# Splitting one long score product in the pair phases and adding met waits on TensorE: a causal attention layer on one core

## Chip, cores and metric

The kernel runs on one core of a Trainium2 chip. The metric is the device time of one execution in microseconds; lower is better. The engines are named as the profile names them: PE (TensorE matmuls), PEld (its weight loads), ACT, DVE, POOL and SP (which issues transfers).

## The reference

The input is x of 32 x 256 x 32 x 32 in float32, that is 32 batches of 256 channels and 1024 positions. It is normalised in 32 groups of 8 channels, then goes through a causal attention of 8 heads of 32 channels without the diagonal, and the result is added to x.

```python
q = jnp.einsum('oc,bcs->bos', q_w, xf) + q_b[None, :, None]
kv = jnp.einsum('oc,bcs->bos', kv_w, xf) + kv_b[None, :, None]
...
mask = jnp.tril(jnp.ones((S, S), dtype=x.dtype), -int(MASK_CENTER))
scores = jnp.einsum('bhqd,bhkd->bhqk', q, k) / jnp.sqrt(jnp.asarray(dk, x.dtype))
scores = jnp.where(mask == 0, jnp.asarray(-10000.0, x.dtype), scores)
attn = jax.nn.softmax(scores, axis=-1)
attn = jnp.where(mask == 0, jnp.asarray(0.0, x.dtype), attn)
out = jnp.einsum('bhqk,bhkd->bhqd', attn, v)
...
x = x + _L0_conv_ref(_gn(x), L0_conv_q_w, L0_conv_q_b, L0_conv_kv_w, L0_conv_kv_b)
```

## The kernel before

A batch is worked through in 12 visits: two groups `g` of four heads, six visits each (the table `VISITS`). Everything is unrolled, and the order of instructions on each engine is that of the program, written out by hand in the loop over `i` at the end: visit `i` of batch `b` issues the scores of this visit, then what stands in the list `at` for it (one projection unit of this or the next batch), then the products with the values of the visit before (`values`), then sums of exponentials on DVE and other small work.

Scores. Keys stand on the partitions of the result, queries in its columns. Each product (`score`, L311) has 32 rows (one head's channels) and 64 keys, so that four heads (row groups) and two halves of a key block (column groups) make eight parts of the array. A visit has "longs", made by `full`, of up to 512 query columns, and "shorts". In six visits (numbers 1, 3, 4, 7, 9, 10) there is one long of 512 columns, and the shorts are a `pair`: two key blocks on the diagonal, each half in two products, of 128 and of 64 columns. Visits 0 and 6 are pairs as well, with two longs, of 384 and 128 columns. Three PSUM tiles take a visit's scores: `pairs[0]` (longs of heads 0, 1), `pairs[1]` (longs of heads 2, 3) and `pairs[2]` (all shorts).

Order within the scores (`scores`, from L348). First the shorts of heads 2, 3 (`first`); where the visit is in `PAIRS` and has two longs, one long of heads 0, 1 is put between its two parts and the parts are turned round (L364, L365). Then what remains of the longs of heads 0, 1 (`begin`), then a long of heads 2, 3. Then PE waits for the semaphore `bank_free`, which the last products of `first` raise, because the shorts of heads 0, 1 write the same banks; then these shorts. ACT takes the exponentials of the three tiles into SBUF (L397, L393), and POOL masks the diagonal ones (L339).

Projections. A unit is `project_qk` (a half of q or k for a group: two times four matmuls of 512 columns, `product`, L169, tile pp) or `project_v` (four times four matmuls of 256 columns, tile ppv). A batch has twelve units, one a visit, dealt by `PROJECT`; by the visit's number they are q or k in visits 7, 8, 10, 0, 1, 2, 5, 6 and v in 9, 11, 3, 4. `product` makes four matmuls of 32 result rows each, one for each column group of the array.

Values. `values` (L422) makes three or four times four matmuls of 128 to 512 columns into the tile acc.

Small work that PE has besides: `norm_mean` (tile pm, behind the values of visit 3) and `norm_variance` (pv, visit 4) for a later batch. SP waits for `bank_free` in `with_scores` to time some of its transfers. `ALIGN` places drains on DVE and 64 met waits on POOL (L669) at the start of the program. The semaphore `arrived` is at 1 or above from the load of the weights on.

## Time and profile before

| | |
|---|---|
| time, median of 3 runs | 1793.67 us (1793.61 to 1793.85) |
| the profiled execution's own time | 1793.44 us |
| its span, first to last instruction | 1791.7 us |
| granted TensorE clock, mean | 0.999 |
| PE busy | 1784.4 us, 37,036 matmuls |
| PEld busy | 948.2 us, 37,036 loads |
| DVE busy | 1673.4 us |
| ACT busy | 1456.4 us |
| POOL busy | 881.3 us |

A float32 matmul of the program stands in the trace as two, each with a weight load of its own, so counts of matmuls are twice those of the code. In the groups of instructions, `L311 PE MATMUL sT<-q,k 32*64 32x128` is a matmul from line 311 into tile sT, with 32 rows and 64 columns of weights and 128 moving columns. "x" gives the count, then follow busy time and mean length. A matmul's start is measured, its end is modelled. "Idle before" is time in which the engine did nothing ahead of the instruction, with what ended it; for PEld this is no loss, since loads run beside matmuls. In a table of stretches, each row is a stretch from A to B, its length, and for an engine the busy time and in brackets the number of instructions under way in it, then the granted clock, the share of the DMA engines and their rate. Sequencer instructions such as waits (EVENT_SEMAPHORE) have records but count as neither busy nor idle.

### The profile page before, as it was taken

What the parts mean: (1) busy time and instruction counts of PE and PEld (TensorE: products, weight loads), DVE (VectorE), ACT (ScalarE), POOL (GpSimd) and SP (SyncE); (2) the same over time, 40 slices, a digit from 0 to 9 for tenths busy, and PEclk for the clock granted to TensorE, in tenths of its full rate; (3) what the DMA queues carried; (4) which work ended last, traced back from release to release, by engine and by line L of the source; (5) the groups of instructions that cost most, each with busy time, mean ns of one, the idle gap of its engine ahead of it and who ended that gap; (6) DMA issues with size and microseconds to landing.
All of it is one profiled execution on the core that took longest, in us unless ns stands there. A gap on an engine that the chain in (4) does not pass through costs nothing.

```text
span 1791.7 us, 81825 instructions
## 1 busy us (share of the span) xinstructions
PE 1784.4 (100%) x37036; PEld 948.2 (53%) x37036; DVE 1673.4 (93%) x1826; ACT 1456.4 (81%) x1990; POOL 881.3 (49%) x903
## 2 busy tenths in 40 slices
PE   9999999999999999999999999999999999999998
PEld 5555555555555555555555555555555555555554
DVE  4689999999999999999999999999999999999998
ACT  6888878888788888788887888878888878888785
POOL 2345544554545555445554455454555544555452
PEclk9999999999999999999999999999999999999999
DMA  2566766767667766766676676767776667666664
GB/s 70 105 115 137 134 134 129 147 135 143 127 126 149 140 138 134 135 139 138 139 135 131 129 150 132 145 125 128 149 141 135 136 134 138 139 139 137 132 107 106
DMA packets 86818, 236.77 MB, mean 132 GB/s; under 512 B 21312, under 2 KB 22336, under 8 KB 70592
## 3 DMA queue, kind: packets, MB, share of 16 engines
q0 software_dynamic: 15872, 97.53, 40.1%
q1 hardware_dynamic: 70448, 133.89, 25.5%
q8 instruction: 290, 4.75, 1.1%
q14 instruction: 64, 0.52, 0.1%
q10 hardware_dynamic: 144, 0.07, 0.0%
HBM read 66.85 MB, written 34.57 MB: 57 GB/s over the span
## 4 chain that ended last, share of the span: by engine, by line
PE 99%; ACT 0%; DVE 0%; issue 0%; POOL 0%; POOLq 0%
PE sT L311 31%; PE acc L422 28%; PE pp L169 26%; PE ppv L169 13%; PE pd L474 1%; PE busy L155 0%; ACT e L397 0%; PE pv L169 0%; PE pm L169 0%; PE wt L148 0%; DVE rb_last L547 0%; ACT eh L393 0%; DVE rb_last L534 0%; DVE turned L531 0%; DVE acc L544 0%
## 5 line engine op out<-in xcount | busy, mean ns | idle before, releaser
L339 POOL TENSOR_SCALAR_AFFINE_SELECT diagonal<-eh 128x512 f32<-128x512 f32 x512 | 632.5, 1256 | 841.5 <-ACT eh L393 840.9
L397 ACT ACTIVATE e<-sT 128x1024 f32<-128x1024 f32 x768 | 744.4, 1022 | 250.3 <-PE sT L311 225.9
L440 DVE TENSOR_TENSOR e<-e,e 128x1024 f32<-128x1024 f32 x314 | 574.2, 1829 | 24.5 <-ACT v L275 3.2
L311 PE MATMUL sT<-q,k 32*64 32x128 f32 (+2 forms) x18432 | 578.4, 372 | 0.1
L311 PEld LDWEIGHTS sT<-q,k 32*64 32x64 f32 x18432 | 394.8, 131 | 188.4 <-PE sT L311 69.6
L169 PE MATMUL pp<-xn,wT 128*32 128x512 f32 x4096 | 492.2, 598 | 0.0
L422 PE MATMUL acc<-e,v 128*32 128x512 f32 (+3 forms) x4608 | 401.0, 450 | 0.0
L393 ACT ACTIVATE eh<-sT 128x768 f32<-128x768 f32 (+1 forms) x384 | 341.7, 890 | 0.0
L422 PEld LDWEIGHTS acc<-e,v 128*32 128x32 f32 x4608 | 149.2, 110 | 261.5 <-issue 238.9
L169 PE MATMUL ppv<-wT,xn 128*32 128x256 f32 x4096 | 247.5, 382 | 0.0
L440 DVE TENSOR_TENSOR diagonal<-diagonal,e 128x1536 f32<-128x1536 f32 x126 | 195.0, 1548 | 16.8 <-PE acc L422 9.2
L169 PEld LDWEIGHTS pp<-xn,wT 128*32 128x32 f32 x4096 | 107.0, 109 | 195.7 <-issue 163.7
L440 DVE TENSOR_TENSOR e<-e,eh 128x1024 f32<-128x1024 f32 x126 | 164.2, 1303 | 6.5
L422 PEld LDWEIGHTS acc<-diagonal,v 128*32 128x32 f32 x4096 | 121.1, 110 | 87.6 <-issue 76.0
L440 DVE TENSOR_TENSOR e<-e,diagonal 128x2048 f32<-128x2048 f32 x63 | 144.2, 2289 | 19.8 <-POOL diagonal L339 19.8
L169 PEld LDWEIGHTS ppv<-wT,xn 128*32 128x32 f32 x4096 | 120.1, 109 | 79.7 <-issue 7.0
L422 PE MATMUL acc<-diagonal,v 128*32 128x128 f32 x4096 | 158.7, 273 | 0.0
L244 ACT ACTIVATE xn<-x,shift,rstd 128x256 f32<-128x256 f32 x248 | 136.8, 608 | 0.6 <-POOL shift L229 0.6
L544 DVE TENSOR_TENSOR num<-num,rb 128x512 f32<-128x512 f32 x124 | 123.3, 994 | 0.2 <-DMA rb<-inverses 0.2
L453 POOL DMA_DIRECT2D e<-e x124 | 103.3, 833 | 38.2 <-issue 38.2
L547 DVE SCALAR_TENSOR_TENSOR rb<-num,v_bias_col,x 128x256 f32<-128x256 f32 x248 | 117.5, 515 | 4.4
L453 POOL DMA_DIRECT2D diagonal<-diagonal x124 | 104.1, 839 | 4.8 <-issue 4.8
(84 smaller groups left out, 984.4 us busy)
## 6 DMA issues: line engine op xcount, KB each, us to landing
x<-in_x_dram SPq DMA_DIRECT2D x124, 256.0 KB, 3.7
diagonal<-diagonal POOLq DMA_DIRECT2D x62, 512.0 KB, 5.4
e<-e POOLq DMA_DIRECT2D x62, 512.0 KB, 5.9
rb<-inverses SPq DMA_DIRECT2D x124, 256.0 KB, 3.9
out_dram<-rb SPq DMA_DIRECT2D x124, 256.0 KB, 4.9
diagonal<-diagonal POOLq DMA_DIRECT2D x62, 256.0 KB, 4.6
folded<-diagonal SPq DMA_DIRECT2D x62, 256.0 KB, 5.1
e<-e POOLq DMA_DIRECT2D x62, 256.0 KB, 5.0
```

The costliest lines, as they stand in the source:

```text
L169: nc.tensor.matmul(out[part], lhsT=lhsT[:, part], rhs=rhs, start=start, stop=stop, skip_group_check=True)
L244: nc.scalar.activation(to, of, AF.Identity, bias=live["shift", b][:, g : g + 1], scale=rstd)
L311: return nc.tensor.matmul(bank[c : c + KEYS, cols], lhsT=live["k", b, g][rows, kb * P + c : kb * P + c + KEYS], rhs=live["q", b, g][rows, ...
L339: nc.gpsimd.affine_select(out=square[:, :, place + s * P : place + (s + 1) * P], in_=raw[:, :, (1 - s) * KEYS : (3 - s) * KEYS], pattern=[ ...
L393: exp = nc.scalar.activation(eh.rearrange("p (n bank) q -> p bank n q", n=2)[:, :, :, :narrow], short[:, :, :, :narrow], AF.Exp)
L397: nc.scalar.activation(e[:, 2 * a : 2 * a + 2, :wide], pairs[a][:, :, :wide], AF.Exp)
L422: nc.tensor.matmul(acc[HD * j : HD * (j + 1), of], lhsT=live["v", b][:, kb, h * HD : (h + 1) * HD], rhs=e[:, j, :], start=first, stop=last ...
L440: nc.vector.tensor_add(to, to, tile_of(b, g, at))
L453: nc.gpsimd.dma_start(out=total[:rows], in_=total[rows : 2 * rows], accum_op=ALU.add)
L474: nc.tensor.matmul(pd[HD * j : HD * (j + 1), of], lhsT=pick, rhs=e[:, j, :], start=start, stop=stop, skip_group_check=True,)
L544: nc.vector.tensor_mul(num, num, rb)
L547: nc.vector.scalar_tensor_tensor(blocks(rb, s), blocks(num, s, (start + s) % 2 == 1), v_bias_col[:, g : g + 1], blocks(xt[:, g, cols], s), ...
```

## The change

Two things are changed. In the visits of `SPLIT` (1, 3, 4, 7, 9, 10, the six pairs with one long), the long of heads 0, 1 is issued in two pieces by `part_of`: columns 0 to 128 and columns 128 to 512. `begin` then has two entries, so that the branch of L364 is taken: the shorts of heads 2, 3 come with their second part first, the piece of 128 columns stands between their parts, and the piece of 384 columns follows them. The long of heads 2, 3 and the shorts of heads 0, 1 are as they were.

And `fill(k)` puts waits on PE for the semaphore `arrived`, which has long been reached, behind each group of four matmuls of a projection: twice the number that `FILL` has for this visit's place in the batch and the group's place `k` in the unit. It does so from visit 6 of the program on, there with `EXTRA` = 7 more. The numbers of `FILL` add up to 158, so that a batch has 316 wait statements.

```diff
+        def fill(k):
+            i = live.get("visit", -1)
+            if i >= SKIP:
+                for _ in range(2 * (sum(FILL[i % N][k : k + 1]) + EXTRA * ((i, k) == (SKIP, 0)))):
+                    nc.tensor.wait_ge(live["arrived"], 1)
...
@@ project_qk, behind each of the two products
+                fill(cc)
...
@@ project_v, behind each of the four products
+                    fill(NG * s + cc)
...
+        def part_of(b, g, bank, entry, of):
+            at, _, halves = entry
+            for j in (0, 1):
+                for ((c, kb, first, _, cols),) in halves:
+                    score(b, g, bank[:, j, :], j, (
+                        c, kb, first + of.start, of.stop - of.start, slice(cols.start + of.start, cols.start + of.stop)
+                    ))
...
-            if i in PAIRS and len(longs) > 1:
+            if v in SPLIT:
+                begin = [lambda n=n: part_of(b, g, pairs[0], longs[0], n) for n in (slice(0, P), slice(P, HALF))]
+            if i in PAIRS and len(begin) > 1:
                 first = short_of((2, 3), begin.pop(0), slice(None, None, -1))
             else:
                 first = short_of((2, 3))
...
+        SPLIT = 1, 3, 4, 7, 9, 10
...
+        FILL = ((8, 8), (8, 8), (8, 8), (4, 4, 4, 4), (3, 4, 4, 2), (1, 8), (8, 8), (8, 8), (8, 8), (0, 0, 0, 0), (0, 8), (4, 4, 4, 4))
+        SKIP, EXTRA = 6, 7
...
             for i in range(B * N + 1):
+                live["visit"] = i
                 if i < B * N:
                     scores(*divmod(i, N))
```

## The prediction

> **What bounds the kernel.** I read the page first: busy time and the chain that ended last.

> ```profile
> PE 1784.4 (100%) x37036; PEld 948.2 (53%) x37036; DVE 1673.4 (93%) x1826; ACT 1456.4 (81%) x1990; POOL 881.3 (49%) x903
> ...
> PE 99%; ACT 0%; DVE 0%; issue 0%; POOL 0%; POOLq 0%
> PE sT L311 31%; PE acc L422 28%; PE pp L169 26%; PE ppv L169 13%; PE pd L474 1%; PE busy L155 0%; ACT e L397 0%; PE pv L169 0%; PE pm L169 0%; PE wt L148 0%; DVE rb_last L547 0%; ACT eh L393 0%; DVE rb_last L534 0%; DVE turned L531 0%; DVE acc L544 0%
> ```

> TensorE is the chain, in three phases a visit: scores (sT), a projection (pp or ppv), products with the values (acc). The view of PE's waits holds 3.0 us in all, at the two ends of the run, so no engine is waited for in between. ACT ends the three exponentials of a visit at least 160 ns before the next visit overwrites their banks (visits 2 and 8; elsewhere 0.3 us or more). A saving on PE is therefore a saving in the end, and so is a loss.

> Next, the timeline of the weight loads over two visits of batch 12, columns start, length, what. The first visit is number 0, which already has its phases interleaved; the second is number 1, a pair without.

> ```profile
> 679.84 0.58 PEld L311 LDWEIGHTS sT<-q,k 32*64 32x64 f32 x40 [0.20 <-ACT v L275]
> 681.26 0.16 PEld L169 LDWEIGHTS pp<-xn,wT 128*32 128x32 f32 x8
> 684.41 0.54 PEld L311 LDWEIGHTS sT<-q,k 32*64 32x64 f32 x32 [0.41 <-ACT k L258]
> 685.81 0.16 PEld L169 LDWEIGHTS pp<-xn,wT 128*32 128x32 f32 x8
> ```

> The score phase takes 1.42 us in visit 0 and 1.40 in visit 1 (1419 and 1403 ns to the nanosecond). Over batches 2 to 29 every visit repeats within 2 ns; a batch is 55.09 us. Visits 1, 3, 7, 9, 10 have 1403 ns of scores, visit 4 has 1411. Third, matmuls of L311 under way in small windows from the start of each phase:

> ```profile
> 679.84:679.87 0.03, 0.02 (x4) 1.00 0.00 0
> 679.84:679.90 0.06, 0.05 (x8) 1.00 0.00 0
> 684.41:684.43 0.03, 0.02 (x4) 1.00 1.31 328
> 684.41:684.46 0.05, 0.05 (x4) 1.00 1.04 287
> 684.41:684.49 0.09, 0.08 (x8) 1.00 0.96 265
> ```

> Heads 2, 3 begin at 1 ns in both. Heads 0, 1, on other rows of the array, have begun within 55 ns in visit 0 (single starts: 28 to 48 ns), but in visit 1 not by 50 ns (55 to 75). That lag is what the first part of the change can take.

> [...] in visit 1 heads 0, 1 are 32 instructions behind the first of heads 2, 3 in the program, yet start before heads 2, 3 make their second pass at 162 ns. [...] from the end of the last score stream to the next phase's first load are 88 ns, in visits 0, 1 and 2 alike. [...]

> ```profile
> q8 instruction: 290, 4.75, 1.1%
> ```

> That is 16.4 KB a packet, and 290 times 256 is 74,240, near PE's 74,072 loads and matmuls. [...]

> **Part 1, the split, 192 times (6 visits, 32 batches).** Four products of 512 columns become four of 128 and four of 384: 48 more matmuls and 48 more loads a batch as the trace counts them (two passes for each). Columns stay the same. The order becomes that of visit 0: 64 columns of heads 2, 3; 128 of heads 0, 1; 128 of heads 2, 3; 384 of heads 0, 1; the long one of heads 2, 3; then the short ones of heads 0, 1 behind the bank_free wait. Two row streams run side by side, and I follow both with visit 0's starts.

> Heads 0, 1. In visit 1 their short products start at 964 ns and the last stream ends at 1258 + 57 = 1315, then 88 of drain: 1403. In visit 0 they start at 942: 27 ns less lag, about 5 lost on the extra passes. With the same 294 + 57 + 88 that makes 1381, a gain of 22.

> Heads 2, 3. In visit 0 the weight loads of their long product stand at places 64 to 79 of the phase, and come at 280, 356, 373, 390 ns for the four tiles, where visit 1, with places 48 to 63, had all four at 329 to 349. So the tiles start at 387, 409, 426, 443 (load to stream 53). At 512 columns the second pass follows 430 later, at 873 for the last, ends at 1303, plus 88 is 1391. This stream now ends last: **the phase is 1391, a gain of 12 ns**. Visit 4, which follows the small product pm, has 8 more of lag in heads 0, 1; I take half of it back. 5 x 12 + 16 = 76 ns a batch, x 32 = 2.43 us. Bounds: 0 (if the later loads slip by another 12) and 28 a visit with visit 4 at 36 (all of the lag, 5.6 us). No gain below nothing is likely: it would need the loads of heads 2, 3 later than in visit 0, whose first 64 instructions are the same.

> Nothing else moves by more: the exponential of heads 0, 1 comes some 20 ns sooner (visit 0: 1188, visit 1: 1210); bank_free rises at 566 instead of 564 ns, so SP's queued loads and stores stay where they were. DVE's and POOL's work hangs on ACT.

> **Part 2, the met waits.** By the diff there are 2 x 158 = 316 wait statements a batch from visit 6 on. On POOL the 64 statements of L669 left 32 records, two waits in each, and PE has single waits at L169:

> ```profile
> L669 POOLq EVENT_SEMAPHORE  x32: 42/43/43, 4.3 to 7.0; - x32
> L169 PEldq EVENT_SEMAPHORE  x67: 51/51/51, 7.2 to 1693.0; - x67
> ```

> So 158 instructions a batch, 31 x 158 + 16 + 7 = 4921 in all. Their spacing on PE is not in the trace. Bounds: 87 ns as on POOL (2.7 us over 31 steps), and 121, adding the 34 by which PE's single record (51) exceeds POOL's (17). I take 87 to 110. What they cost depends on the sequencer's lead. The waits of L169 before pm run 1.70 us ahead of their own matmuls, those before pv 1.27: 36 instructions ahead in both. By that rule the first wait behind a projection's first 16 instructions runs at some 965 ns of the visit, while the array is busy with scores until 1391.

> Visits with q or k: 8 waits, 16 instructions, 8 waits, then the loads of acc, due at about 3024 (110 before acc at 3134, as acc stands 1.74 us behind pp now). Instructions come at 17 ns for four (the steps 356, 373, 390). 965 + 70 + 16 E is below 3024 for E up to 124 ns: **hidden under the projection's 1.74 us**. Visits with v and 16 waits (3, 11): 965 + 270 + 16 E against 3034 (acc 1.75 us behind ppv): hidden up to E = 112. Visit 4 has 13, visit 9 none, 10 has 8: more room. Queued behind the waits are only PE's own loads and matmuls, and ACT, which waits for these; both are late only if the array is. I take nought. If the cover is gone the cost is 16 ns a visit for each ns of E above 112. A gain I exclude: no step of the array waits for a slower sequencer.

> **Fetch.** A batch now has 2306 PE instructions (2304 loads and matmuls, 2 waits), nine blocks and two. With 96 and 158 more it has 2560, ten blocks, so the crossings stay in place from batch to batch. Before they drifted by 2 a batch, and only once did a crossing show: in batch 25, visit 0, five weight loads come 64 ns late, hidden in 84 ns of slack ahead of their matmuls. I book nothing; bound, one exposed crossing a batch, 64 x 31 = 2.0 us. Thirty more fetches of 16 KB on a DMA share of 0.6 to 0.7 are nothing.

> **Sum.** 1793.44 is the profiled execution (span 1791.7, 1.7 around it), 0.23 under the median. 1793.44 - 2.43 = 1791.0; on the median, **1791.2 us**, -0.14%. About 0.2% (3.6 us) is what a measurement of this kernel can tell from no change.

> **Rivals.**
> A, chance 0.48: as above, 1790.0 to 1792.5.
> B, 0.28: the loads of heads 2, 3 don't slip, the whole 22 to 28 ns come: 192 x 22 = 4.2 us, to 5.6: 1788.0 to 1789.5. For it: the slip is seen in visit 0 alone. Against: the same 64 instructions stand before it.
> C, 0.15, slower: waits take over 112 ns each and the queue runs dry in visits 3 and 11. At 121 acc is late by 9 x 16 = 144 ns in each: 2 x 144 x 31 = 8.9 us, less 2.4: 1800. It decides from E = 118 (0.2% slower). Against: POOL's 87. For: PE's longer record.
> D, 0.09: the change doesn't do what it says in time, the lag only moves to the tail of heads 2, 3, or a crossing a batch eats it: 1792.5 to 1795.

> Faster by over 0.2% (under 1790.1) takes B and 0.05 of A: 0.33. Slower (over 1797.3) is C: 0.15. The rest 0.52. The range 1788.0 to 1795.0 leaves out C and the edge of B.

> **What would show it.** Right: score phases of visits 1, 3, 7, 9, 10 at about 1391 ns, heads 0, 1 starting at 28, heads 2, 3 ending last; visits 0, 2, 5, 6, 8, 11 unchanged; batch 55.02 us; some 4921 wait records on PE under 112 ns apart, the lead kept; 38,572 matmuls and about 321 fetches. B: phases near 1381. Wrong: acc starting later after ppv in visits 3 and 11 than the 1.75 us of before (C), or any visit's time varying from batch to batch.

## The result and the profile after

The changed kernel takes 1816.68 us (median of 4, 1813.36 to 1819.98) against 1793.76 us of the kernel before beside it: a ratio of 1.0127, 95% interval 1.0106 to 1.0148. It is 1.3% slower; forecast were 1791.2 us and a range up to 1795.0. The profiled execution took 1818.47 us.

The page of the changed kernel, beside the lines of the same rows in the prediction:

```profile
PE 1799.1 (99%) x38572; PEld 964.2 (53%) x38572; DVE 1669.3 (92%) x1826; ACT 1457.9 (80%) x1990; POOL 869.7 (48%) x903
...
q8 instruction: 322, 5.28, 1.2%
...
PE 99%; issue 1%; ACT 0%; DVE 0%; POOL 0%; POOLq 0%
...
L169 PE MATMUL pp<-xn,wT 128*32 128x512 f32 x4096 | 503.4, 598 | 7.8 <-issue 7.8
```

The last of these groups in the kernel before:

```profile
L169 PE MATMUL pp<-xn,wT 128*32 128x512 f32 x4096 | 492.2, 598 | 0.0
```

PE is still the chain, the counts (38,572 matmuls; 322 packets of instructions for about 321) are as forecast, and yet 1% of the chain is now "issue": PE stood still for nothing that the profile shows. The group of pp has 7.8 us of it where the kernel before had none; its busy time rose too, from 492.2 to 503.4 us, because a matmul's end is modelled and some ends reach into the gap (by 0.59 us from the last start in batch 5 below). So busy and idle together give the loss (19.0 us there), not the idle alone. The waits of PE say where:

```profile
PE pp L169 <- issue: 7.8, 10, 1.1
PE acc L442 <- issue: 2.0, 4, 0.8
```

**The split did what it should.** Timeline of the weight loads in visits 0 and 1 of batch 12, undisturbed here (start, length, what):

```profile
686.06 0.57 PEld L320 LDWEIGHTS sT<-q,k 32*64 32x64 f32 x40 [0.20 <-ACT v L284]
...
687.47 0.16 PEld L169 LDWEIGHTS pp<-xn,wT 128*32 128x32 f32 x8
...
690.62 0.57 PEld L320 LDWEIGHTS sT<-q,k 32*64 32x64 f32 x40 [0.41 <-ACT k L266]
...
692.01 0.16 PEld L169 LDWEIGHTS pp<-xn,wT 128*32 128x32 f32 x8
```

Visit 1 now looks like visit 0: 40 loads at once, and the projection 1.39 us behind the start of the scores. Scores take 1387 ns in the median in all six split visits; before they took 1403, in visit 4 1411. Small windows from the start of the phase, matmuls of L320:

```profile
690.62:690.65 0.03, 0.03 (x4) 0.03 (x4) 1.00 0.44 137
690.62:690.67 0.05, 0.04 (x7) 0.05 (x7) 1.00 0.58 164
```

By 50 ns seven are under way, where the kernel before had four: heads 0, 1 begin at 28 ns instead of 55.

**The waits did what they should.** The instructions of line 251:

```profile
L251 PEldq EVENT_SEMAPHORE  x4921: 51/51/51, 47.8 to 1785.9; - x197
```

4921 records of two waits each, as counted; within a group most of them (3506 of 4273 steps) follow each other by 105 or 106 ns, inside the 87 to 110 taken; the others by up to 146. In an undisturbed visit they cost nothing that shows: a batch without a disturbance takes 54.98 us, against 55.09 before, and 54.98 too when the waits are left out (split_only below).

**But not every batch is undisturbed.** Before, each batch took 55.09 us. Now they take 54.98 to 57.7 us, and the surplus has two places. I take the shortest time of each of the twelve visits as undisturbed, and add up over batches 1 to 30 what the visits have above it ("surplus" from here on): 18.7 us in visit 5, 8.3 in visit 0, 0.7 in all others; 27.7 in all. An undisturbed run would be 1793.44 - 32 x 0.11 = 1789.9 us; with the 27.7 it is 1817.6, of 1818.47 measured.

Here is one disturbed visit 5, that of batch 5: weight loads of PE in the timeline.

```profile
320.47 0.16 PEld L169 LDWEIGHTS pp<-xn,wT 128*32 128x32 f32 x8 [0.20 <-issue]
320.93 0.12 PEld L169 LDWEIGHTS pp<-xn,wT 128*32 128x32 f32 x3 [0.30 <-issue]
321.36 0.12 PEld L169 LDWEIGHTS pp<-xn,wT 128*32 128x32 f32 x3 [0.31 <-issue]
323.17 0.14 PEld L169 LDWEIGHTS pp<-xn,wT 128*32 128x32 f32 x2 [1.69 <-issue]
324.01 0.19 PEld L442 LDWEIGHTS acc<-e,v 128*32 128x32 f32 x8 [0.70 <-issue]
```

Fourteen of the projection's sixteen loads come in their rhythm of 0.43 us, then there is nothing for 1.69 us. In the undisturbed visit 5 of the batch before, the loads are 8, 4, 4, and acc follows at once:

```profile
265.49 0.16 PEld L169 LDWEIGHTS pp<-xn,wT 128*32 128x32 f32 x8 [0.20 <-issue]
265.95 0.13 PEld L169 LDWEIGHTS pp<-xn,wT 128*32 128x32 f32 x4 [0.30 <-issue]
266.38 0.13 PEld L169 LDWEIGHTS pp<-xn,wT 128*32 128x32 f32 x4 [0.30 <-issue]
266.81 0.13 PEld L442 LDWEIGHTS acc<-e,v 128*32 128x32 f32 x4 [0.30 <-issue]
```

The DMA view of the stretch from the start of visit 4 to PE's return, first in the disturbed batch 5 (busy tenths in 40 slices of 0.22 us, where a packet's whole time is put into the slice in which it starts, so that an empty slice isn't a rest; then queues with packets, MB, share of 16 engines; then issues):

```profile
DMA  0000000000930009950000357999999849429200
...
q0 software_dynamic: 48, 0.26, 33.2%
q8 instruction: 1, 0.02, 0.6%
...
e<-e POOLq DMA_DIRECT2D x1, 256.0 KB, 5.3
```

The same 8.9 us of visits 4 and 5 in batch 4:

```profile
q0 software_dynamic: 48, 0.26, 31.6%
q8 instruction: 2, 0.03, 1.7%
...
e<-e POOLq DMA_DIRECT2D x1, 256.0 KB, 5.1
```

Batch 4 has two fetches in this stretch, batch 5 a single one. The trace's records of the packets give the times. In batch 4 the first fetch starts 1.70 us into visit 4, ahead of the packets of the transfer `e<-e` (`fold`, which POOL issues 0.87 us into the visit); these run from 2.26 to 5.65 us. In batch 5 the fetch starts at 6.46 us, when the transfer's packets (2.26 to 5.82) are through. It takes 0.92 us, and PE goes on 1.38 us later, at 323.17.

Over batches 1 to 30 this fetch starts at 1.65 to 4.2 us in nineteen, and visit 5 is undisturbed in all of them. In the other eleven it starts at 5.4 to 6.7 us, in four of them 0.03 to 0.15 us before the last packet of the transfer ends, in seven 0.64 us after, and those are the eleven disturbed visits 5. The transfer has 32 packets of 8 KB and 16 of 4 bytes. In the eleven late cases all 32 have started before the fetch. In eighteen of the nineteen others at most 16 have, so that the fetch may start up to 1.04 us after the first of them (batch 8: 3.26 us); only in batch 1, where POOL issues the transfer 0.8 us earlier, does the fetch stand behind it and yet come in time, at 4.2 us.

The chain of events, as I read it from these times: PE comes to the block of a fetch 4.2 us after the fetch's start in the middle case (5.4 before), counted to the place where the gaps are. In batch 4 the fetch starts 1.70 us into visit 4, and the 29th instruction of the projection, the first behind that place, at 6.96. A fetch that doesn't get ahead of an accumulating transfer starts only when that is nearly or wholly through (the eleven late cases), and where the block in hand doesn't last until about 2.3 us after the fetch's start (2.30 in batch 5), PE stands.

The disturbed visits 0 hang together with those of visit 5. The fetch that counts there stands behind the 512 KB transfer that POOL issues in visit 11. In the eighteen undisturbed cases POOL issues it 1.5 to 2.0 us ahead of visit 0, in the twelve disturbed ones (over 0.1 us of surplus) 2.4 to 3.5 us ahead, so that it is before the fetch. Ten of these twelve are in the batch after a disturbed visit 5, and each of the ten disturbed visits 5 up to batch 29 has such a successor. So most of the loss in visit 0 follows from that in visit 5, and no_fold below bears it out. That PE's delay is what lets POOL be earlier in relation to PE fits, but wasn't tried by itself.

### The profile page after: what moved, and what is told of

Same layout as the page of the kernel before. It is cut to its first block, busy times and chain, and to the rows that moved or that the text cites. A ratio compares the mean times of both kernels' runs of the same rounds, so it can differ in the third digit from the quotient of the medians.

```text
span 1816.7 us, 89818 instructions
## 1 busy us (share of the span) xinstructions
PE 1799.1 (99%) x38572; PEld 964.2 (53%) x38572; DVE 1669.3 (92%) x1826; ACT 1457.9 (80%) x1990; POOL 869.7 (48%) x903
## 4 chain that ended last, share of the span: by engine, by line
PE 99%; issue 1%; ACT 0%; DVE 0%; POOL 0%; POOLq 0%
PE sT L320 30%; PE acc L442 28%; PE pp L169 27%; PE ppv L169 13%; PE pd L494 1%; PE busy L155 0%; ACT e L417 0%; PE pv L169 0%; PE pm L169 0%; PE wt L148 0%; DVE rb_last L567 0%; ACT eh L413 0%; DVE rb_last L554 0%; DVE turned L551 0%; DVE acc L564 0%
## 5 line engine op out<-in xcount | busy, mean ns | idle before, releaser
L357 POOL TENSOR_SCALAR_AFFINE_SELECT diagonal<-eh 128x512 f32<-128x512 f32 x512 | 621.9, 1236 | 877.8 <-ACT eh L413 877.7
L460 DVE TENSOR_TENSOR e<-e,e 128x1024 f32<-128x1024 f32 x314 | 566.7, 1805 | 24.4 <-ACT v L284 3.1
L320 PE MATMUL sT<-q,k 32*64 32x128 f32 (+2 forms) x19968 | 574.7, 356 | 0.3 <-ACT e L417 0.3
L169 PE MATMUL pp<-xn,wT 128*32 128x512 f32 x4096 | 503.4, 598 | 7.8 <-issue 7.8
L320 PEld LDWEIGHTS sT<-q,k 32*64 32x64 f32 x19968 | 401.3, 131 | 177.6 <-PE sT L320 63.1
L169 PE MATMUL ppv<-wT,xn 128*32 128x256 f32 x4096 | 247.5, 382 | 0.0
L169 PEld LDWEIGHTS pp<-xn,wT 128*32 128x32 f32 x4096 | 111.5, 108 | 210.7 <-issue 163.5
L460 DVE TENSOR_TENSOR e<-e,eh 128x1024 f32<-128x1024 f32 x126 | 170.2, 1350 | 6.5
L169 PEld LDWEIGHTS ppv<-wT,xn 128*32 128x32 f32 x4096 | 120.3, 109 | 80.1 <-issue 11.7
```

The lines of the kernel that those rows point to most:

```text
L169: nc.tensor.matmul(out[part], lhsT=lhsT[:, part], rhs=rhs, start=start, stop=stop, skip_group_check=True)
L320: return nc.tensor.matmul(bank[c : c + KEYS, cols], lhsT=live["k", b, g][rows, kb * P + c : kb * P + c + KEYS], rhs=live["q", b, g][rows, ...
L357: nc.gpsimd.affine_select(out=square[:, :, place + s * P : place + (s + 1) * P], in_=raw[:, :, (1 - s) * KEYS : (3 - s) * KEYS], pattern=[ ...
L460: nc.vector.tensor_add(to, to, tile_of(b, g, at))
```

## The experiments

"Surplus" is taken as above. Theory F is this chain. What the first three kernels had to tell apart was the fetch (F), the waits' own time (W) and the new order of the scores (S); from the fourth, no_fold, on the transfer in front of the fetch is tried.

**split_only**: the split without the waits.

```diff
-        FILL = ((8, 8), (8, 8), (8, 8), (4, 4, 4, 4), ...
-        SKIP, EXTRA = 6, 7
+        FILL = ((0, 0),) * 12
+        SKIP, EXTRA = 6, 0
```

> The split of the change with no met waits at all. Theory F (PE stands still because the next block of 256 instructions lands late): 2402 PE instructions a batch, so block ends wander by 98 a batch, blocks last 5.9 us on the mean instead of 5.5: clean batches of 54.98 us, at most a few stalls in single batches, never at one place throughout; 1790 to 1797 us. Theory W (the waits' own time empties PE's queue): no stall at all, 1790.2. Theory S (the new order of the scores stalls PE): stalls in visits 0 and 5 as with the whole change, over 1805.

Measured: 1799.72 us (1797.41 to 1800.28), ratio 1.0028 (1.0017 to 1.004). Undisturbed batches take 54.98 us, so the whole gain of 0.11 us a batch is the split's. The surplus is 9.8 us, mainly in 15 visits whose places move (visits 1, 7, 10), since a batch of 2402 instructions is 9.4 blocks. The time is above the 1790 to 1797 that I had given for F. The split alone thus gains 3.5 us and loses more; W can't be the only cause, there being no waits.

**waits_only**: the waits without the split.

```diff
-        SPLIT = 1, 3, 4, 7, 9, 10
+        SPLIT = ()
```

> The met waits of the change without the split. F: 2464 instructions a batch, block ends wander by 96 a batch and pass the bad places: clean batches as before (55.09 us), stalls of 1 to 2 us at changing places, 1797 to 1812 us. W: the same stalls in visit 5 and 0 as with the whole change, about 1820. S: 1793.7, no stall.

Measured: 1837.76 us (1830.35 to 1845.62), ratio 1.0257 (1.0214 to 1.0299), outside what I had given for F. Undisturbed batches take 55.08 us, what they took before: 158 waits at 105 ns stay hidden. The surplus is 36.9 us, over visits 0, 1, 3, 5, 9, 10 by turns (9.6 blocks a batch). S is out as the cause: the order of the scores is the old one. The block ends wander here, and the loss is larger than in the changed kernel, so that ends fixed in place are not what makes the loss.

**shift79**: everything as in the change, but without the 79 waits of batch 0, once; each later block end lies 79 instructions later in the program.

```diff
-        SKIP, EXTRA = 6, 7
+        SKIP, EXTRA = 12, 0
```

> The whole change, but the 79 met waits of visits 6 to 11 of the first batch left out, so that every later block end lies 79 instructions later in the program while all later visits are instruction for instruction the same. F: no stall in visit 5 behind the first half of pp, nor in visit 0 behind acc; stalls, if any, at the new block ends (visit 4 start of acc, visit 6 start of scores, visit 0 scores place 32, visit 9 end of ppv); another total, 1790 to 1812. W and S: as the whole change, about 1817, with the same stalls in visits 5 and 0.

Measured: 1864.95 us (1859.89 to 1869.94), ratio 1.0385 (1.0362 to 1.0408), 53 us above F's upper figure. Nothing is left in visits 5 and 0. The surplus is 42.2 us in visit 3, 24.6 in visit 9, 10.2 in visit 1, 77.9 in all. In visits 3 and 9 its gaps stand behind the 11th and the 3rd instruction of acc, where block ends now are. PE's waits:

```profile
PE acc L442 <- issue: 31.9, 30, 1.8
...
PE sT L320 <- issue: 0.5, 1, 0.5
```

From batch 1 on every batch has the same instructions, the whole run has 79 waits fewer, and the loss nearly trebles and moves: it hangs on where the blocks end, which neither W nor S says.

**no_fold**: the accumulating transfer of head group 3 that POOL issues in visit 4 is left out (part of the sums of the exponentials is missing).

```diff
-                        when(v + 2 + late, lambda b=b, n=n: fold(b, n, HD), after)
+                        if n < 3:
+                            when(v + 2 + late, lambda b=b, n=n: fold(b, n, HD), after)
```

> The whole change, with the second fold of the last sums of each batch left out (the accumulating transfer that POOL issues in visit 4 of the next batch; the sums of that half are then incomplete). F: the fetch asked for in visit 4 no longer waits behind this transfer, its packet starts within 3.4 us of the visit's start in every batch, visit 5 has its clean 4.63 us in every batch; visit 0 still stalls now and then; about 1800 us, 17 less than the whole change. W and S: about 1817, stalls in visit 5 stay.

Measured: 1796.08 us (1794.12 to 1798.65), ratio 1.001 (1.0001 to 1.0019). Visit 5 falls from 18.7 us to 0.1, visit 0 from 8.3 to 2.0. This is more than I had said (about 1800), in the same direction: with the stalls of visit 5 most of those that follow them in visit 0 go too. The fetch of visit 4 now starts at 4.5 us at the latest.

**two_folds**: that transfer and the 512 KB one of head group 2, issued in visit 11, both left out.

```diff
-                        when(v + 2 * late, lambda b=b, n=n: fold(b, n, 2 * HD), ...)
+                        if n != 2:
+                            when(v + 2 * late, lambda b=b, n=n: fold(b, n, 2 * HD), ...)
-                        when(v + 2 + late, lambda b=b, n=n: fold(b, n, HD), after)
+                        if n != 3:
+                            when(v + 2 + late, lambda b=b, n=n: fold(b, n, HD), after)
```

> The changed kernel with two of the eight accumulating transfers a batch left out (the 512 KB one of head group 2 in visit 11, the 256 KB one of head group 3 in visit 4), so the denominators are incomplete. Theory F (a fetch of PE's next 256 instructions that is queued behind such a transfer comes late): the stalls behind the first half of pp in visit 5 (18.7 us) and in the acc of visit 0 (8.3 us) both go; 1790.0 to 1792. Rival T (any traffic delays the fetch, the stores and loads as much as the folds): visit 0 keeps most of its stalls, 1796 to 1800. Rival W (the waits' own time empties the queue): 1813 to 1820.

Measured: 1791.63 us (1790.82 to 1792.57), ratio 0.9986 (0.9979 to 0.9993). A surplus of 0.9 us is left of 27.7, with all split visits and all 158 waits in place. PE's waits have a single line of issue left:

```profile
PE pp L169 <- issue: 0.4, 1, 0.4
```

So the loss at these places needs these two transfers: six others a batch remain, and stores and loads as well. W is out. Other traffic still delays the fetch of visit 4, which starts at 1.6 to 4.5 us here, but not for long enough to matter.

**no_stores**: the two stores of the output a batch that SP issues in visit 4 are left out (half of the output stays unwritten); the transfer stays.

```diff
-   later = None if late else lambda send, ...: when(*((first + 2 * N + 4, send) if n < 2 else (v + 1, send, after)))
+   later = None if late else lambda send, ...: None if n < 2 else when(v + 1, send, after)
```

> The changed kernel with half of its stores of the output left out, the two of 256 KB a batch that are issued in visit 4 (they stay unwritten); the accumulating transfer of visit 4 stays. Theory F in its narrow form (the accumulating transfer alone delays the fetch): visit 5 keeps its stalls, 1810 to 1819. Rival T (any traffic): they go for the greater part, 1795 to 1803.

Measured: 1833.51 us (1824.66 to 1837.16), ratio 1.021 (1.0178 to 1.0242). Visit 5 has 26.0 us of surplus now, in 15 batches instead of eleven:

```profile
PE pp L169 <- issue: 11.1, 14, 1.0
PE acc L442 <- issue: 2.0, 5, 0.5
```

The figure is above F's range too, but less traffic with more stalls says that it isn't traffic as such that holds the fetch. The surplus is 38.4 us in all. Why the fetch loses its race against the transfer more often here stays open.

**shift41**: the block ends moved again, by 41 instructions.

```diff
-        SKIP, EXTRA = 6, 7
+        SKIP, EXTRA = 3, 10
```

> The changed kernel with 41 more met waits once, in batch 0 (SKIP, EXTRA = 3, 10), everything else the same: each end of a block of 256 instructions moves 41 instructions earlier for all the batches after it, to visit 0 between the halves of pp, visit 1 acc 40, visits 3, 4 and 5 at instruction 71 to 75 of the scores, visit 6 between the halves, visit 7 acc 16, visit 9 scores 48, visit 10 scores 80, visit 11 in the third product of v. Theory F: from the start times of the fetches in the five kernels traced so far, every block lasts longer than its fetch takes (by 0.3 us or more) but for that of visits 4 to 5, short by up to 1.0 us, and that of visits 9 to 10, short by up to 0.9: most stalls go, those that stay are in the scores of visits 5 and 10; 1791 to 1800. Rivals W and S (waits, or the new order of the scores, make the loss): as the changed kernel, 1813 to 1820.

Measured: 1812.39 us (1806.74 to 1815.7), ratio 1.0093 (1.0071 to 1.0116). Visit 5's surplus is gone, but visit 0 has 11.6 us, visit 10 has 4.5, visit 11 3.1; 20.0 in all. The size is a miss, and the total alone would fit W as well; the visits don't. Two reasons are in the working of the expectation: its places are eleven instructions too early (the gaps in visits 5 and 0 fix the count), and it took the slowest twelfth of too few fetches for the worst case.

**fold_early**: the transfer of visit 4 issued one visit earlier by the program.

```diff
-   when(v + 2 + late, lambda b=b, n=n: fold(b, n, HD), after)
+   when(v + 2 + late, lambda b=b, n=n: fold(b, n, HD), at if n == 3 else after)
```

> The changed kernel with one accumulating transfer moved and none left out: that of head group 3 (256 KB), which POOL issues 0.9 us into visit 4, is issued in visit 3, behind POOL's mask there, as soon as the 512 KB one before it has landed. It should then land some 2 us before the block end of visit 4 is felt in visit 5. Theory F: the stalls of visit 5 go for the greater part, those of visit 0 (8.3 us) stay: 1797 to 1802. Rival T or W: 1812 to 1820, since traffic and waits are the same. A loss from POOL's standing longer: DVE would be late and visits of other places longer, none expected.

Measured: 1823.87 us (1819.66 to 1828.62), ratio 1.0158 (1.0141 to 1.0175), with 21.0 us of surplus in visit 5. The edit didn't do what it says: POOL is still at its mask of visit 3 when visit 4 begins, and the transfer goes out about 0.87 us into visit 4 in most batches, as before. It tells nothing on F.

**halved**: the two transfers that two_folds left out, each issued in two halves a visit apart.

```diff
-            nc.gpsimd.dma_start(out=total[:rows], in_=total[rows : 2 * rows], accum_op=ALU.add)
+            nc.gpsimd.dma_start(out=total[:rows, heads], in_=total[rows : 2 * rows, heads], accum_op=ALU.add)
...
+   for k, heads in enumerate((slice(0, 2), slice(2, 4)) if n == 2 else (slice(0, 4),)):
+       when(v + 2 * late + k, lambda b=b, n=n, heads=heads: fold(b, n, 2 * HD, heads), at if late else after)
+   for k, heads in enumerate((slice(0, 2), slice(2, 4)) if n == 3 else (slice(0, 4),)):
+       when(v + 2 + late + k, lambda b=b, n=n, heads=heads: fold(b, n, HD, heads), at if k else after)
```

> The changed kernel, complete, with the two accumulating transfers that two_folds left out each issued as two of half the size a visit apart (the 512 KB one as 2 x 256 KB from visit 11 on, the 256 KB one as 2 x 128 KB from visit 4 on). Theory F (a fetch waits for the accumulating transfer ahead of it to get through): the fetch of visit 4 waits for 128 KB instead of 256 and starts at most some 3 us after its block end, which its block of 5.3 us allows; stalls of visit 5 go from 18.7 us to under 6, those of visit 0 (behind 256 KB now, as the others) to under 5: 1792 to 1801. Rival (the delay does not follow the bytes ahead but the mere presence of such a transfer): as many or more stalls, 1812 to 1822.

Measured: 1861.28 us (1858.63 to 1863.62), ratio 1.0373 (1.0355 to 1.039). The total is a miss for F, and far above the rival's range as well. At visits 5 and 0 what F says is seen: the half's packets run from about 2.25 to 4.1-4.8 us of visit 4, the fetch now starts at 5.3 us at the latest (6.7 in the changed kernel), and the surplus falls to 8.5 us in visit 5 and 3.1 in visit 0, though 8.5 is above the 6 that I had given and visit 5 is disturbed in 15 batches instead of eleven. But 16.5 us appear in visit 7, 10.3 in visit 8, 15.6 in visit 11, 4.9 in visit 10; visit 7 is moreover late by 0.3 us or more in every batch, which the surplus doesn't count. The chain is no longer PE's alone:

```profile
PE 82%; POOL 6%; ACT 5%; DVE 3%; issue 2%; DMA 1%; POOLq 0%; SPq 0%; DVEq 0%; ACTq 0%
```

And POOL waits, in its own queue, for the first half to land:

```profile
POOL diagonal L473 <- DMA diagonal<-diagonal: 48.3, 21, 3.2
```

The scores of visit 7, 1387 ns in the changed kernel, take 2.2 us here in the median and up to 2.6. That the waiting POOL is what delays them by way of its masks and ACT fits the chain, but was not tried by itself.

**dealt**: the same 158 waits a batch, dealt out otherwise over the visits; the block ends lie elsewhere.

```diff
-   FILL = ((8, 8), (8, 8), (8, 8), (4, 4, 4, 4), (3, 4, 4, 2), (1, 8), (8, 8), (8, 8), (8, 8), (0, 0, 0, 0), (0, 8), (4, 4, 4, 4))
-   SKIP, EXTRA = 6, 7
+   FILL = ((5, 8), (8, 8), (8, 8), (4, 4, 4, 3), (0, 0, 1, 1), (0, 0), (8, 8), (8, 8), (8, 8), (4, 4, 4, 4), (8, 8), (4, 4, 4, 4))
+   SKIP, EXTRA = 8, 0
```

> The changed kernel with the same 158 met waits a batch dealt out otherwise: 13, 16, 16, 15, 2, 0, 16, 16, 16, 16, 16, 16 for visits 0 to 11 from visit 8 of batch 0 on. It puts the block ends at visits 1, 2, 7, 8 in the scores, 3 and 9 and 10 in the projections, 4, 5 and 11 in acc. Only the position changes. Theory F: the start times of the fetches in the runs so far make the blocks begun in visits 3 to 4 short by up to 1.0 us and that of visit 11 short by up to 0.5, all others long enough; stalls at most some 10 us in all, 1790 to 1802, and none behind the first half of pp in visit 5. Rival W (the waits' time): as the changed kernel or worse where visits now have 16 (9, 10), 1812 to 1825.

Measured: 1802.35 us (1798.9 to 1804.08), ratio 1.0043 (1.0026 to 1.006). The surplus is 10.3 us, 7.9 of it in visit 1, 0.6 in visit 5. With the same number of waits a batch the time is 14 us shorter, in the direction that the fetch times gave and just above F's range; the place of the largest rest was missed. The visits have other numbers of waits here, so that the place of the block ends is not all that differs.

**dealt_halved**: both edits.

> Both edits, of dealt and of halved, together; complete. Theory F: no more stalls than in the better of the two, 1790 to 1797; if it comes under 1792.5 it beats the kernel before. Rival: as in the two.

Measured: 1870.47 us (1862.55 to 1874.31), ratio 1.0413 (1.0386 to 1.0439). A miss for F as I had written it. Visits 5 and 0 have no disturbance left, but visits 10 and 11 lose 35 us, and visit 7 takes at least 1 us more than in the changed kernel in every batch: the losses that come with halving outweigh what either edit saves.

**thirty**: 30 waits a batch, so that a batch is nine and a half blocks.

```diff
-   FILL = ((8, 8), (8, 8), (8, 8), (4, 4, 4, 4), (3, 4, 4, 2), (1, 8), (8, 8), (8, 8), (8, 8), (0, 0, 0, 0), (0, 8), (4, 4, 4, 4))
-   SKIP, EXTRA = 6, 7
+   FILL = ((1, 1), (2, 2), (8, 8), (0, 0, 0, 0), (0, 0, 0, 0), (0, 0), (0, 0), (0, 0), (3, 3), (0, 0, 0, 0), (1, 1), (0, 0, 0, 0))
+   SKIP, EXTRA = 5, 9
-   ... EXTRA * ((i, k) == (SKIP, 0))
+   ... EXTRA * (i < N and k == 0)
```

> The changed kernel, complete, with 30 met waits a batch instead of 158 (2, 4, 16 in visits 0 to 2, 6 in visit 8, 2 in visit 10; 63 more once in batch 0 to set the place). A batch is then 2432 PE instructions, nine and a half blocks of 256, so the block ends alternate between two places from batch to batch, and a block lasts 5.8 us on average instead of 5.5; the before had 6.1. Theory F (a stall is a block that lasts less than its fetch is late): from the fetch starts so far the shortest blocks are short by up to 1.0 us in a slow twelfth or less of the cases, three places in two batches; the loss over a clean run (1790.2) is 1 to 9 us, 1791 to 1799, less than for dealt. If it came under 1792.5 it would beat the kernel before. Rival W (each wait costs its time on the array): from 158 to 30 waits takes four fifths of the loss of dealt's 12 us as of the changed kernel's 26, 1792.5 to 1796, and no visit would vary from batch to batch.

Measured: 1797.54 us (1793.81 to 1802.07), ratio 1.0019 (1.0013 to 1.0026). Undisturbed batches 54.98 us, a surplus of 6.1 us in visits 9 and 10 of some batches; W said that no visit would vary. It is the best complete kernel with the split, and still behind the kernel before.

The time is the median; the surplus is that of the profiled execution alone. fold_early and the kernels with halved transfers or without stores are left out here.

| kernel | us | surplus, us | in visits |
|---|---|---|---|
| before | 1793.76 | none | |
| changed | 1816.68 | 27.7 | 5, 0 |
| shift79 | 1864.95 | 77.9 | 3, 9, 1 |
| shift41 | 1812.39 | 20.0 | 0, 10, 11 |
| dealt | 1802.35 | 10.3 | 1 |
| thirty | 1797.54 | 6.1 | 9, 10 |
| split_only | 1799.72 | 9.8 | 1, 10, 7 |
| waits_only | 1837.76 | 36.9 | 0, 5, 10, 3, 1 |
| no_fold (part left out) | 1796.08 | 3.4 | 0 |
| two_folds (part left out) | 1791.63 | 0.9 | |

## Why the prediction was wrong

**Part 1 held.** 12 ns a phase were forecast, 16 measured, 24 in visit 4 where I had 16: 104 ns a batch by the phases, 110 by the batches, against 76. The picture behind the 12 fits as well: in visit 1 of batch 12 the second passes of the long product of heads 2, 3 now start at 817 to 871 ns (873 forecast for the last; 817 to 837 before). By the modelled ends this stream now ends last, at 1458 ns against 1454 for heads 0, 1, where before heads 0, 1 did, at 1477 against 1424. By this part alone the kernel would have been at about 1790.2 us on the median, at the lower edge of rival A.

**Part 2 held.** 4921 records, mostly 105 ns apart, hidden; rival C's condition of over 112 ns each was not met, and its places (visits 3 and 11) were not where the loss came. That the first wait runs early enough was right in undisturbed visits. That a met wait takes no time of the array was an estimate of mine; undisturbed batches take 54.98 us with 158 of these instructions and with none (split_only).

**The step that failed is "Fetch".** It had the counts right and even saw that with 2560 instructions "the crossings stay in place from batch to batch". It drew the wrong conclusion from both. Three errors are in it:

- It priced a crossing by the 64 ns of the one late fetch in the trace of before. Those 64 ns were no price but the tip of one: the rest of the delay lay in the time that the block in hand still lasted. With 1.4 us from the packet's end to PE (1.38 in batch 5 above, 1.31 to 1.56 in the twelve stalls of over 1 us), I estimate from the fetches' records that the least time to spare of any fetch of before is 0.3 us, the middle one 3.1; in the changed kernel the middle one is 1.8, and the surplus of the 24 disturbed visits is 0.1 to 2.1 us, not 64 ns.
- It took the mean load of the DMA engines (0.6 to 0.7) as proof that 30 more small packets don't matter. One transfer in front of it was enough to hold a fetch up: in batch 5 it starts 4.8 us later than in batch 4, with the DMA engines busy for 0.71 of the stretch shown above against 0.68.
- It took "in place" for harmless. Before, the block ends drifted by two instructions a batch, some 60 in the whole run, and a block lasted 6.1 us (55.09 over nine). Now a block lasts 5.5 us, and in every batch the same two block ends can meet the same two transfers. A fixed place can be a good one or a bad one: between 1802 and 1865 us in the four kernels with 2560 instructions and all transfers whole (dealt, shift41, the changed kernel, shift79). Whether the kernel before owes its calm to the longer blocks or to where its ends lie was not tried: no run moved the block ends of that kernel and kept their number.

The bound of "one exposed crossing a batch", 2.0 us, took the same 64 ns and so was fourteen times too small. The last sentence of the prediction had named the sign, "any visit's time varying from batch to batch", and that is what came. Most of the 320 crossings are hidden here too; the 24 visits with over 100 ns of surplus cost 1.5% of the run.

## What to carry to other kernels

On an engine that is the bound all the time, the number of instructions can be a cost even where each is hidden (27.7 us here): count the fetches in the trace (here one for 256 instructions), divide the time by them, and compare with how late a fetch can be, not how late it is on average. Look up each fetch's packet and its time to spare before its block is needed. Here the smallest was about 0.3 us, and every complete kernel with more instructions a batch had stalls. If batches repeat, see which transfers start beside the block ends, above all accumulating ones (without two of these the surplus here was 0.9 us, without two stores 38.4), since adding instructions anywhere ahead moves all of the block ends (41 and 79 waits did so here).

## What the runs showed of the hardware

- A fetch of 16 KB that didn't get ahead of an accumulating transfer from SBUF to SBUF started at about the end of it: in the eleven late cases of visit 4 from 0.15 us before the end of its last packet to 0.64 us after. In batch 5 the packets of the 256 KB transfer start in three groups of sixteen some 1.2 us apart (8 KB each from 316.67 and 317.87 us, 4 bytes each from 319.15 us); the first sixteen take 1.2 to 1.4 us each. The fetch comes behind all of them, 4.8 us later than in batch 4. In 16 of the 18 batches where the fetch gets ahead of its transfer, one of the transfer's 8 KB packets starts within 17 ns of the fetch's end. What puts the two in this order was not shown: the records don't name the engine of a packet.
- The transfer's packets of 8 KB take 0.84 us in the median, the 2 KB packets of SP's transfers 0.08. Whether the size of the packets or the accumulating is what makes these transfers hold a fetch was not tried.
- In ten of the twelve disturbed visits 0 the fetch starts 20 or 21 ns before the end of a last packet of such a transfer, in the other two 0.8 and 1.0 us after.
- From the start of a fetch's packet to PE's next instruction are 2.3 to 2.7 us in the twelve stalls of over 1 us, of which the packet takes 0.9 to 1.2.
- Two met waits in one instruction cost PE's sequencer mostly 105 or 106 ns from start to start, though the record shows 51.
